# One RWKV block on one core: new landing estimates in a hand-built plan, and a new order of all pieces

## The chip, the cores and the metric

One NeuronCore of one Trainium2 chip. The time is that of one execution of the whole program on the device, in microseconds; lower is better. The core's engines are TensorE (PE, its weight loads are listed as PEld), VectorE (DVE), ScalarE (ACT), GpSimd (POOL) and SyncE (SP), which here only issues transfers.

## The reference, cut to what matters

Eight sequences (`b`) of 256 tokens with 512 channels (32 heads of 16) go through one RWKV block, in float32:

```python
xn = _ln(x, ln1_w, ln1_b);  sx = _token_shift(xn, state[:, i1])
xxx = jnp.tanh((xn + sx * maa_x) @ maa_w1).reshape(b, l, 5, 1, EXTRA_MAA)
xxx = jnp.matmul(xxx, maa_w2).reshape(b, l, 5, E)
x5 = xn[:, :, None] + sx[:, :, None] * (maa_stack + xxx)
w = jnp.exp(-jnp.exp(time_decay + jnp.tanh(x5[:, :, 1] @ decay_w1) @ decay_w2))
r, k, v = x5[:, :, 3] @ Wr.T, x5[:, :, 0] @ Wk.T, x5[:, :, 2] @ Wv.T
g = jax.nn.silu(x5[:, :, 4] @ Wg.T)
def step(s, rkvw):                       # over the 256 tokens
    a = k_t[:, :, :, None] * v_t[:, :, None, :]
    out = jnp.einsum('bhk,bhkd->bhd', r_t, u * a + s)
    return (a + w_t[:, :, :, None] * s, out)
att = group_norm(outs) * gn_w + gn_b
x = x + att * g @ Wo.T
xn2 = _ln(x, ln2_w, ln2_b);  sx2 = _token_shift(xn2, state[:, i0])
rr = jax.nn.sigmoid((xn2 + sx2 * ffn_maa_r) @ ffn_Wr.T)
kk = jnp.square(jax.nn.relu((xn2 + sx2 * ffn_maa_k) @ ffn_Wk.T))
return x + rr * (kk @ ffn_Wv.T)
```

## The kernel before, in words

The program is a list of 2,633 **pieces** of work, each of a few instructions on one engine: 397 for PE, 1,132 for ACT, 479 for DVE, 374 for POOL and 251 transfers. For every sequence the pieces come in three stages. `inputs_of_scan` normalizes the input, transposes it (L614), mixes it with the shifted one (`psx`, the small `tanh` part and the mixing matmuls `psm`, whose results DVE and POOL turn into five mixed inputs at L716, L720 and L726) and makes the projections k, v, r and g (`psk`, `psv`, `psr`, `psg`, by `project`, all matmuls through `mul` at L430) and the decay (`psd` at L766, `psw`). `scan` runs the recurrence in four blocks of heads with four quarters each. For a quarter the values come back broadcast from DRAM (`vs<-vo`; `vo` is written by two small transfers on ACT's queue at L816 for sequence 0 and by one at L866 for the others), DVE multiplies them with k (L889; POOL at L886 for a few), DVE scans (L891), POOL multiplies with r (L894), and PE sums the four quarters of a block into one tile, `pat`, which is called the gather below (L902; 32 matmuls that begin with one of each quarter). `rest` makes the group norm (squares at L920, means `pv` at L928, logarithm and exponential on ACT at L933 and L935, for the last sequence a spread by matmuls at L943), the gate (L959, L968), the output projection `pso` with the residual on DVE (L974), the second layer norm (L556, L595, L598) with its transposes `psT2` (L614), and the two feed-forward projections `psfk`, `psfr` and `psfv` (ACT at L983, L984, L992; DVE at L1015; POOL's last sum at L1020).

The order is not written out in the functions. Each piece is added with a cost and, for a transfer, with a time on the wire and a lag until it has landed (`EARLY` for named first transfers, `LANDS` by kind, else a default). `sequence` gives each piece its rank from the table `TURNS`, one number for each piece, stage by stage. `order` then takes the pieces by rank as soon as what they need is placed, gives each the latest-freed fitting buffer out of its pool, and works out starts from the costs; the pieces are emitted sorted by these starts, and each engine executes its own in that order. So a landing figure moves no transfer by itself: it changes the starts that `order` works out, and by them the sorting and the buffers. All transfers go through `dma` (L419) on SP's queue, except the writes of `vo`. Six tiles of PSUM (`ps`) serve all projections, gathers and transposes. ACT has two sets of function tables, one with the exponential and one with tanh and silu; where a piece needs the other set, L1048 puts a table load ahead of it.

The lines that speak of landings are these:

```python
op.wire, op.lag = self.EARLY.get(name) or self.LANDS.get("".join(c for c in name if not c.isdigit()), (kb / 370, 1.5))
...
landed = wire = max(wire, op.start + 1.0) + op.wire
...
o.ready = max(o.ready, op.end + op.gap if same else landed + op.lag + self.AHEAD.get(o.engine, 0.0))
```

Of the kernel before, what the change touches and what calls it, by code (L numbers as in the profile page):

```python
# [70 lines left out]
class Plan:  # L71
# [7 lines left out]
    EARLY = {"xt0_0": (0.76, 0.8), "xt0_1": (0.76, 0.8), "cen": (0.35, 1.5), "vec": (0.2, 1.5), "xt1": (1.4, 1.5), "xt2": (1.4, 1.5), "Wfr0_1": (1.4, 1.5),  # L79
             "Wraw0": (1.65, 1.5), "Wraw1": (1.65, 1.5)}  # L80
# [23 lines left out]
    def add(self, engine, us, outs, ins, emit, mode=None, into=(), lag=0.0, kb=0, part=False):  # L104
# [7 lines left out]
        if kb:  # L112
            name = op.bufs[0].name
            op.wire, op.lag = self.EARLY.get(name) or self.LANDS.get("".join(c for c in name if not c.isdigit()), (kb / 370, 1.5))

# [17 lines left out]
    def stage(self):  # L133
# [990 lines left out]
```

## Time and profile before

| | before |
|---|---|
| median of three runs | 608.50 us (608.11, 608.50, 608.68) |
| the profiled execution, its own time | 608.87 us |
| its span from the first to the last instruction | 607.1 us |
| busy: PE, DVE, ACT, POOL | 597.6, 531.2, 513.3, 505.4 us |
| bytes moved, mean rate | 124.85 MB, 206 GB/s |
| granted clock of TensorE | 1.00 throughout |

The profile's page gives busy time and shares of the span for each engine, then the chain of work that ended last, then the costliest groups of instructions. The timeline lists instructions in order of time; in brackets stands how long the engine sat idle before one, and what released it. "SPq" and "ACTq" are transfers issued by these engines.

### The profile page before, as it was taken

The numbers are of one execution on the slowest core, as the hardware profiler recorded it, in microseconds if no ns is written. First come the engines' busy times: TensorE is split into PE (matmuls) and PEld (weight loads), VectorE is DVE, ScalarE is ACT, GpSimd is POOL, SyncE is SP. The second block draws the span as 40 slices with busy tenths as digits, with TensorE's granted clock in tenths as the row PEclk, the third lists the DMA queues.
The fourth block names the chain that finished last, engine by engine and source line by source line (L and its number), as shares of the span: only waits on it lengthen the run. The fifth ranks groups of instructions, "written<-read, shape, count | busy, mean of one in ns | idle before, by whom it ended". The sixth has DMA issues, their size and how long they took to land.

```text
span 607.1 us, 18838 instructions
## 1 busy us (share of the span) xinstructions
PE 597.6 (98%) x7892; PEld 344.4 (57%) x7892; DVE 531.2 (87%) x481; ACT 513.3 (85%) x1199; POOL 505.4 (83%) x385
## 2 busy tenths in 40 slices
PE   8999999999999999999999999999999999999997
PEld 7575655467444574377544774465644454745464
DVE  6699999899999989799798999999999999994332
ACT  4898879999999999999999999999998688963431
POOL 1699999999989897899979898989989989887030
PEclk9999999999999999999999999999999999999999
DMA  9796688898778868486589597795876798961551
GB/s 292 251 246 163 143 205 207 223 263 219 205 210 252 231 189 231 138 233 174 164 256 238 143 270 219 225 228 148 271 212 174 204 252 220 265 194 43 177 185 65
DMA packets 52500, 124.85 MB, mean 206 GB/s; under 512 B 5824, under 2 KB 11200, under 8 KB 52416
## 3 DMA queue, kind: packets, MB, share of 16 engines
q1 hardware_dynamic: 48048, 119.46, 71.8%
q10 hardware_dynamic: 4368, 4.20, 2.2%
q8 instruction: 62, 1.02, 0.7%
q14 instruction: 22, 0.18, 0.1%
HBM read 115.25 MB, written 8.39 MB: 204 GB/s over the span
## 4 chain that ended last, share of the span: by engine, by line
PE 88%; ACT 6%; DMA 4%; DVE 2%; issue 1%; SPq 0%; DVEq 0%; ACTq 0%
PE ps L430 73%; PE ps L902 9%; PE ps L614 2%; PE ps L766 2%; DMA Wk<-in_wk 2%; ACT ps L714 1%; DMA mw2a<-in_maa_w 1%; ACT sq L957 1%; DMA x<-in_x 1%; PE ps L928 1%; ACT L1048 1%; PE ps L844 1%; ACT rk L957 1%; ACT mix L984 0%; DVE x L974 0%
## 5 line engine op out<-in xcount | busy, mean ns | idle before, releaser
L891 DVE TENSOR_TENSOR_SCAN st<-wrep,vs 128x1024 f32<-128x1024 f32 x128 | 288.9, 2279 | 4.3 <-ACT wrep L872 2.2
L894 POOL TENSOR_TENSOR st<-st,r 128x1024 f32<-128x1024 f32 x128 | 254.2, 2002 | 11.3 <-DVE st L891 10.4
L889 DVE TENSOR_TENSOR vs<-vs,ps 128x1024 f32<-128x1024 f32 x122 | 144.6, 1208 | 9.3 <-ACT vs L882 6.5
L430 PE MATMUL ps<-Ws,mix 128*32 128x512 f32 (+2 forms) x804 | 114.7, 589 | 0.5 <-DVE x L974 0.2
L430 PEld LDWEIGHTS ps<-Ws,mix 128*32 128x32 f32 (+1 forms) x804 | 38.8, 118 | 62.7 <-issue 55.6
L726 POOL TENSOR_TENSOR mix<-mix,xn 128x512 f32<-128x512 f32 x62 | 67.0, 1096 | 7.7 <-DVE mix L720 6.8
L902 PE MATMUL ps<-st,con 128*32 128x256 f32 x1024 | 62.6, 380 | 0.3 <-DVE x L974 0.2
L430 PE MATMUL ps<-mix,Wg 128*32 128x256 f32 (+1 forms) x784 | 60.2, 379 | 0.3 <-ACT mix L983 0.2
L430 PE MATMUL ps<-mix,Wv 128*32 128x256 f32 (+1 forms) x832 | 59.9, 380 | 0.2 <-DVE mix L723 0.2
L430 PE MATMUL ps<-mix,Wr 128*32 128x256 f32 (+1 forms) x688 | 59.9, 380 | 0.0
L430 PE MATMUL ps<-mix,Wk 128*32 128x256 f32 (+1 forms) x880 | 59.4, 380 | 0.2 <-DMA Wk<-in_wk 0.2
L430 PE MATMUL ps<-mix,Ws 128*32 128x256 f32 (+1 forms) x784 | 58.2, 379 | 0.0
L430 PE MATMUL ps<-Ws,g 128*32 128x512 f32 (+1 forms) x416 | 57.1, 593 | 0.0
L1048 ACT ACT_TABLE_LOAD x39 | 50.0, 1283 | 1.1 <-ACT v L797 0.4
L647 POOL TENSOR_TENSOR mix<-mix,xn 128x512 f32<-128x512 f32 x44 | 47.2, 1093 | 3.1 <-ACT mix L645 2.9
L430 PEld LDWEIGHTS ps<-mix,Wr 128*32 128x32 f32 (+1 forms) x688 | 39.3, 123 | 17.9 <-issue 1.4
L714 ACT ACTIVATE ps<-ps,vec 128x256 f32<-128x256 f32 x112 | 45.7, 445 | 4.2 <-PE ps L430 2.7
L430 PEld LDWEIGHTS ps<-mix,Wv 128*32 128x32 f32 (+1 forms) x832 | 37.9, 116 | 19.5 <-issue 1.1
L902 PEld LDWEIGHTS ps<-st,con 128*32 128x32 f32 x1024 | 34.1, 110 | 26.3 <-issue 5.1
L430 PEld LDWEIGHTS ps<-mix,Ws 128*32 128x32 f32 (+1 forms) x784 | 39.6, 118 | 16.4 <-DVE mix L640 0.6
L430 PEld LDWEIGHTS ps<-mix,Wg 128*32 128x32 f32 (+1 forms) x784 | 38.4, 118 | 18.2 <-issue 1.0
L430 PEld LDWEIGHTS ps<-mix,Wk 128*32 128x32 f32 (+1 forms) x880 | 36.8, 114 | 20.6 <-issue 2.4
(116 smaller groups left out, 935.3 us busy)
## 6 DMA issues: line engine op xcount, KB each, us to landing
vs<-vo SPq DMA_DIRECT2D x128, 512.0 KB, 5.6
Ws<-in_wo SPq DMA_DIRECT2D x16, 512.0 KB, 6.6
Ws<-in_fr SPq DMA_DIRECT2D x16, 512.0 KB, 6.0
Ws<-in_fk SPq DMA_DIRECT2D x16, 512.0 KB, 5.6
Ws<-in_fv SPq DMA_DIRECT2D x16, 512.0 KB, 4.7
x<-in_x SPq DMA_DIRECT2D x9, 512.0 KB, 6.4
vo<-v ACTq DMA_DIRECT2D x15, 256.0 KB, 4.9
out<-o SPq DMA_DIRECT2D x15, 256.0 KB, 4.6
```

Source lines behind the costliest of these rows:

```text
L430: nc.tensor.matmul(out[i : i + n], lhsT=w[:, i : i + n], rhs=x, start=first, stop=final)
L614: nc.tensor.transpose(ps()[:, m, n * P : (n + 1) * P], xh[n]()[:, k * P : (k + 1) * P], idt())
L647: gp(512, t, [t, xn[q]], lambda q=q, t=t: nc.gpsimd.tensor_tensor(t(), t(), xn[q]()[:, :, 1 : T + 1], ALU.add))
L714: act(256, p_, [p_, vec], lambda g=g, q=q, m=m, p_=p_: nc.scalar.activation(p_()[:, m, :], p_()[:, m, :], AF.Identity, bias=col(f"maa_{g}" ...
L726: gp(512, t, [t, xn[q]], lambda q=q, t=t: nc.gpsimd.tensor_tensor(t(), t(), xn[q]()[:, :, 1 : T + 1], ALU.add))
L766: nc.tensor.matmul(pd()[i : i + 32, 0, :], lhsT=w, rhs=src[k // 2]()[:, k % 2, :], start=(k == begin), stop=(k == end))
L889: dve(4 * T, [vs], [vs, kp], lambda m=m, vs=vs, kp=kp: nc.vector.tensor_tensor(vs(), vs(), kp()[:, m : m + 1, :].to_broadcast([P, 4, T]), ...
L891: dve(4 * T, [st], [w, vs], lambda w=w, vs=vs, st=st: nc.vector.tensor_tensor_scan(st().rearrange("p n t -> p (n t)"), w().rearrange("p n ...
L894: gp(4 * T, st, [st, r], lambda m=m, st=st, r=r: nc.gpsimd.tensor_tensor(st(), st(), r()[:, m : m + 1, :].to_broadcast([P, 4, T]), ALU.mul ...
L902: nc.tensor.matmul(pat()[32 * i : 32 * i + 32, 0, :], lhsT=con()[:, s : s + 32], rhs=done[i]()[:, j, :], start=(j == 0), stop=(j == 3),)
L957: act(256, rsb, [rs], lambda blk=2 * q + n, n=n, rows=rows, rsb=rsb: nc.scalar.copy(by_block(rsb)[rows, n, :], rs()[32 * blk : 32 * blk + ...
L1048: nc.scalar.preload_act_table_set(TABLES[table])
```

## The change

Landing figures of the first transfers are set anew, and the whole table of ranks is replaced. Pieces, costs, pools and buffers stay as they were.

```diff
-    EARLY = {"xt0_0": (0.76, 0.8), "xt0_1": (0.76, 0.8), "cen": (0.35, 1.5), "vec": (0.2, 1.5), "xt1": (1.4, 1.5), "xt2": (1.4, 1.5), "Wfr0_1": (1.4, 1.5),
-             "Wraw0": (1.65, 1.5), "Wraw1": (1.65, 1.5)}
+    EARLY = {"xt0_0": (0.76, 1.28), "xt0_1": (0.76, 1.2), "cen": (0.35, 2.1), "vec": (0.2, 2.3), "xt1": (1.4, 2.3), "xt2": (1.4, 2.0), "idt": (0.17, 2.4), "Wfr0_1": (1.4, 1.5),
+             "Wraw0": (1.65, 2.1), "Wraw1": (1.65, 2.0)}
...
-            op.wire, op.lag = self.EARLY.get(name) or self.LANDS.get("".join(c for c in name if not c.isdigit()), (kb / 370, 1.5))
+            op.wire, op.lag = self.EARLY.get(name) or self.LANDS.get("".join(c for c in name if not c.isdigit()), (kb / 370, 2.0))
...
     TURNS = """
-        11 45 15 38 49 98 95 96 109 46 94 72 220 97 55 62 64 140 16 14 26 20 27 43 18 54 58 17 40 48 19 60 61,
+        3 66 13 39 57 92 67 93 99 69 58 68 70 198 107 108 120 121 9 18 24 21 32 44 19 60 61 20 30 43 33 51 55,
...
```

Three places show what the new ranks do. First SP's queue at the head of the program; names are the destinations (`Wk_74` and `Wk_73` are the two halves of the k weights, `xt_85` the input of sequence 1, `vs` the first broadcast values). Before, from the twelfth transfer on:

```order
L419 DMA mw2a<-in_maa_w 128x512
L419 DMA s_81<-in_state 128x64
L419 DMA s_82<-in_state 128x64
L419 DMA xt_85<-in_x 128x2x512
L419 DMA Wr_78<-in_wr 128x2x512
L419 DMA Wr_77<-in_wr 128x2x512
L419 DMA dw_69<-in_decay_w 128x4x64
L419 DMA dw_70<-in_decay_w 128x512
L419 DMA Wg_80<-in_wg 128x2x512
L419 DMA mw2b<-in_maa_w 128x512
L419 DMA Wk_73<-in_wk 128x2x512
L419 DMA vs_144<-vo_141 128x1x1024
```

Now, from the same place:

```order
L419 DMA mw2a<-in_maa_w 128x512
L419 DMA Wr_77<-in_wr 128x2x512
L419 DMA xt_85<-in_x 128x2x512
L419 DMA con<-in_consts 128x448
L419 DMA dw_69<-in_decay_w 128x4x64
L419 DMA Wr_78<-in_wr 128x2x512
L419 DMA Wk_74<-in_wk 128x2x512
L419 DMA Wg_79<-in_wg 128x2x512
L419 DMA mw2b<-in_maa_w 128x512
L419 DMA dw_70<-in_decay_w 128x512
L419 DMA Wk_73<-in_wk 128x2x512
L419 DMA vs_144<-vo_141 128x1x1024
```

The twenty-two transfers ahead of the first `vs` are the same kinds and sizes in both orders; the first half of Wk goes from eleventh to eighteenth, and the second half stays last.

Second, PE ahead of the gather of sequence 1's second block, after which the transposes of sequence 0's second layer norm stand (the sixteen rows L902 are the 32 matmuls of the gather, then eight rows L614 follow). Before:

```order
L430 MATMUL ps_174<-w_133,dw_70 32x256 x4
L430 MATMUL ps_169<-w_133,dw_70 32x256 x4
L430 MATMUL ps_174<-w_133,dw_70 32x256 x4
L430 MATMUL ps_169<-w_133,dw_70 32x256 x4
L430 MATMUL ps_170<-mix_119,Wk_73 32x256 x8
L430 MATMUL ps_170<-mix_112,Wk_74 32x256 x8
L902 MATMUL ps_172<-st_152,con 32x256
L902 MATMUL ps_172<-st_154,con 32x256
L902 MATMUL ps_172<-st_155,con 32x256
```

Now:

```order
L430 MATMUL ps_173<-w_133,dw_70 32x256 x4
L430 MATMUL ps_170<-w_133,dw_70 32x256 x4
L430 MATMUL ps_173<-w_133,dw_70 32x256 x4
L430 MATMUL ps_170<-w_133,dw_70 32x256 x4
L430 MATMUL ps_169<-mix_119,Wk_73 32x256 x8
L430 MATMUL ps_169<-mix_117,Wk_74 32x256 x8
L430 MATMUL ps_171<-mix_108,Wv_75 32x256 x8
L430 MATMUL ps_171<-mix_107,Wv_76 32x256 x8
L902 MATMUL ps_169<-st_152,con 32x256
L902 MATMUL ps_169<-st_154,con 32x256
L902 MATMUL ps_169<-st_155,con 32x256
```

One half of a v projection (`mix` by `Wv`), which stood behind the transposes, now stands ahead of the gather; gather and transposes follow each other as before.

Third, POOL ahead of the gather of sequence 4's second block, which needs the four products L894 of that block (the last of the four is the last row of each piece). Before:

```order
L858 TENSOR_TENSOR att_140<-v_128,att_140 128x2x256
L726 TENSOR_TENSOR mix_107<-mix_107,xn_98 128x512
L959 TENSOR_TENSOR att_138<-att_138,rk_150 128x2x256
L968 TENSOR_TENSOR g_136<-att_139,g_136 128x512
L968 TENSOR_TENSOR g_137<-att_138,g_137 128x512
L726 TENSOR_TENSOR mix_110<-mix_110,xn_98 128x512
L894 TENSOR_TENSOR st_152<-st_152,r_125 128x1024
L726 TENSOR_TENSOR mix_108<-mix_108,xn_98 128x512
L726 TENSOR_TENSOR mix_106<-mix_106,xn_99 128x512
L726 TENSOR_TENSOR mix_112<-mix_112,xn_99 128x512
L858 TENSOR_TENSOR att_138<-v_129,att_138 128x2x256
L894 TENSOR_TENSOR st_153<-st_153,r_125 128x1024
```

Now:

```order
L726 TENSOR_TENSOR mix_108<-mix_108,xn_99 128x512
L968 TENSOR_TENSOR g_137<-att_138,g_137 128x512
L959 TENSOR_TENSOR att_139<-att_139,rk_150 128x2x256
L726 TENSOR_TENSOR mix_106<-mix_106,xn_99 128x512
L968 TENSOR_TENSOR g_136<-att_139,g_136 128x512
L726 TENSOR_TENSOR mix_107<-mix_107,xn_98 128x512
L894 TENSOR_TENSOR st_153<-st_153,r_127 128x1024
L726 TENSOR_TENSOR mix_110<-mix_110,xn_99 128x512
L1020 TENSOR_TENSOR o_163<-o_163,x_160 128x512
L1020 TENSOR_TENSOR o_162<-o_162,x_160 128x512
L726 TENSOR_TENSOR mix_117<-mix_117,xn_98 128x512
L894 TENSOR_TENSOR st_152<-st_152,r_127 128x1024
```

Two of the last sums of an earlier sequence (L1020) and one mixing sum more (L726) now stand ahead of the block's last product, and of the two multiplications by v (L858) one has gone ahead of this stretch and one behind it. On PE one half of a projection that stood ahead of this gather stands behind it now.

## Rows read from the trace of the kernel before

**Rows 1.** The page: busy time by engine, and the chain's shares by engine.
```profile
PE 597.6 (98%) x7892; PEld 344.4 (57%) x7892; DVE 531.2 (87%) x481; ACT 513.3 (85%) x1199; POOL 505.4 (83%) x385
...
PE 88%; ACT 6%; DMA 4%; DVE 2%; issue 1%; SPq 0%; DVEq 0%; ACTq 0%
```
**Rows 2.** Stretches: from:to, length, busy (count) PE PEld DVE ACT POOL, clock, DMA, GB/s.
```profile
0.00:25.00 25.00, 21.63 (x196) 17.29 (x200) 17.28 (x41) 15.25 (x39) 8.44 (x19) 1.00 0.88 293
...
60.00:90.00 30.00, 30.00 (x592) 18.15 (x588) 30.00 (x25) 23.03 (x51) 29.91 (x19) 1.00 0.71 173
...
540.00:607.00 67.00, 62.88 (x479) 34.64 (x478) 28.34 (x38) 24.43 (x49) 23.28 (x19) 1.00 0.36 126
```
**Rows 3.** Stretches of the head, same columns.
```profile
12.00:15.00 3.00, 2.89 (x22) 2.27 (x29) 2.00 (x8) 2.87 (x5) 0.00 (x0) 1.00 1.07 369
```
**Rows 4.** The chain that ended last, by time: start, us, what.
```profile
15.39 9.36 DMA Wk<-in_wk
...
210.72 3.45 PE ps L430 x64
...
318.19 1.93 PE ps L902 x32
```
**Rows 5.** Timeline of the head, PE and ACT's queue: start, us, engine line.
```profile
7.52 1.06 PE L614 MATMUL ps<-idt,xh 128*128 128x128 f32 x8 [0.97 <-DMA idt<-in_consts]
...
24.86 0.40 PEld L430 LDWEIGHTS ps<-mix,Wk 128*32 128x32 f32 x12 [0.68 <-POOL mix L726]
24.89 0.64 PE L430 MATMUL ps<-mix,Wk 128*32 128x256 f32 x8 [0.22 <-DMA Wk<-in_wk]
...
22.38 0.35 ACTq L816 DMA_DIRECT2D vo<-v  x1
```
**Rows 6.** Timeline at sequence 0's second layer norm.
```profile
128.51 2.52 PE L902 MATMUL ps<-st,con 128*32 128x256 f32 x32
129.11 1.43 PEld L902 LDWEIGHTS ps<-st,con 128*32 128x32 f32 x26 [0.48 <-POOL st L894]
129.24 1.52 ACT L598 ACTIVATE xh<-x,nm,rs 128x512 f32<-128x512 f32 x2
...
130.96 1.09 PE L614 MATMUL ps<-idt,xh 128*128 128x128 f32 x8
```
**Rows 7.** Timeline ahead of the gather of sequence 4's second block, POOL, DVE and PE.
```profile
313.34 1.09 POOL L959 TENSOR_TENSOR att<-att,sq 128x512 f32<-128x512 f32 x1 [2.07 <-ACT sq L957]
...
318.62 1.09 POOL L858 TENSOR_TENSOR att<-v,att 128x512 f32<-128x512 f32 x1 [0.27 <-ACT att L852]
...
323.55 1.09 POOL L968 TENSOR_TENSOR g<-att,g 128x512 f32<-128x512 f32 x1 [0.57 <-ACT att L963]
...
331.81 2.01 POOL L894 TENSOR_TENSOR st<-st,r 128x1024 f32<-128x1024 f32 x1
...
328.13 0.68 DVE L1015 SCALAR_TENSOR_TENSOR o<-o,ps 128x512 f32<-128x512 f32 x1
...
336.61 1.72 PE L902 MATMUL ps<-st,con 128*32 128x256 f32 x28
```
**Rows 8.** Table loads on ACT: the page's group, then the timeline of the last sequence's norm.
```profile
L1048 ACT ACT_TABLE_LOAD x39 | 50.0, 1283 | 1.1 <-ACT v L797 0.4
...
559.18 0.47 ACT L933 ACTIVATE sq<-ps,eh 128x256 f32<-128x256 f32 x1 [1.00 <-PE ps L928]
...
559.69 0.42 ACT L935 ACTIVATE sq<-sq 128x256 f32<-128x256 f32 x1
...
560.76 0.73 PEld L943 LDWEIGHTS ps<-sq,con 64*128 64x128 f32 x8 [0.84 <-ACT sq L935]
```
**Rows 9.** Who waited for whom on PE: total us, times, longest.
```profile
PE ps L614 <- DVE xh L588: 0.5, 1, 0.5
PE ps L430 <- DVE mix L716: 0.4, 1, 0.4
PE ps L430 <- ACT k L797: 0.3, 1, 0.3
```

236 rows, old and new, of the table TURNS are left out of this document.

## The prediction, made before the changed kernel was run

> **What bounds the kernel now.** I read the page first, then stretches of the span, then the chain, then the timeline where the order changes.
>
> The page says that PE is busy for 597.6 of 607.1 us, and that the chain of work that ended last runs through PE for 88% [rows 1]. The other engines are at 83 to 87%. So PE's stream of matmuls is the bound, and an order can only win or lose what PE waits. The 9.5 us in which PE is idle lie mostly at the two ends: 3.4 us in the first 25 us and 4.1 us in the last 67 us [rows 2]; the 515 us between hold 2.0 us. That is not all PE loses, because a wait for operands inside a group is partly booked as busy. The pace without waits is seen in 64 matmuls that take 3.45 us, and in a gather of 32 after which the next group starts 1.93 us later [rows 4]. A place where it takes longer is a stall.
>
> In the first 90 us there is a second bound. DVE is busy for 30.00 of the 30 us from 60 to 90 [rows 2], with the scans of sequence 0. What PE gained ahead of them it would wait for again at the gathers.
>
> The head is bound by transfers. From 12 to 15 us the queues move 369 GB/s at a DMA share of 1.07 [rows 3]; the second half of Wk, issued at 15.39, is in flight for 9.36 us [rows 4], and at 24.89 PE starts the k projection, for which it last waited on that landing, while its weight load waited 0.68 us for a mixing sum of POOL [rows 5].
>
> The sum is made against the profiled execution: 608.87 us, of which 607.1 are span and 1.77 lie around it. It stands 0.37 us above the median of 608.50; the change that I work out is applied to the median.
>
> **The change, part by part.**
>
> *The landing figures themselves: nothing.* They are arithmetic in the planner. No transfer is issued, sized or queued differently because of them; only the order that comes out counts.
>
> *PE's amount of work: nothing.* Both orders have 1,375 rows on PE, with the same pieces, and both change tile shape 82 times.
>
> *The head: nothing, bounds -0.3 and +0.7 us.* The same twenty-two transfers stand ahead of the broadcasts, and the second half of Wk stays last, so behind a saturated queue it lands when all these bytes have. Moved ahead are idt, the centering constant and vec, smaller and earlier. The first transposes waited 0.97 us for idt [rows 5] and may come some tenths sooner, but PE's pieces up to the k projection are the same set, and that projection still waits for the last transfer. What is won before it is waited for there. The gain ends where the mixing sum of POOL ends, 0.3 us earlier at most: the weight load at 24.86 was free to go only then. The loss side is another queue. Two writes of `vo` of 128 KB go out on ACT's queue, the first at 22.38 [rows 5]. In the new order the two halves of the v projection that feed them stand next to each other, so both can be issued about a microsecond earlier, into the last bytes of Wk: 2 x 128 KB at 369 GB/s is 0.7 us if they go wholly first, nothing if they go behind. I take nothing, the nearer end by the row: the first write was issued 2.4 us ahead of that landing before as well. "DMA: Bandwidth & Descriptors", section "Queues, rings and completion order", of the Trainium skill says that each DMA engine takes turns between its queues packet by packet, so the writes would not stand behind Wk; by it an estimated half of the 0.7 us would be lost, and no row of the trace before shows the two side by side.
>
> *The scans of sequence 0: nothing.* DVE is the bound there [rows 2], and it has the same work ahead of the last of these scans in both orders.
>
> *Sequence 0's second layer norm: -0.4 us, bounds -0.5 and +0.3.* The gather starts at 128.51; its next weight loads wait 0.48 us for POOL's last product, and the transposes behind it start at 130.96 [rows 6]. That is 2.45 us where 1.93 are needed [rows 4], so 0.52 us are lost. Now half a v projection, 32 of the matmuls that take 3.45 us for 64, so 1.73 us, stands ahead of the gather. POOL has one multiplication by v more ahead of its last product, 1.09 us by the same line in [rows 7], so product and gather still come within tenths of each other; and the normalized rows that the transposes need, ready at 129.24 + 1.52 = 130.76 [rows 6], are pushed by about 1 us by POOL's small sum and by an eviction on ACT, to about 131.9, against the 132.2 at which PE now gets there. Most of the 0.52 comes back; if POOL is late by another half microsecond, nothing does and 0.3 is lost.
>
> *Sequence 4's second gather: +0.5 us, bounds 0 and +0.9.* POOL's last product ended at 331.81 + 2.01 = 333.82 and the gather started at 336.61, 2.79 us later [rows 7]. In the new order PE arrives 1.73 us earlier, at 334.88, since half a projection has moved behind. POOL has two L1020 and one L726 more, one L858 less between its start at 313.34 and that product: 2 x 1.09, less overlap of neighbours, is 2.1 us. It sat idle for 0.27 and 0.57 us on the way [rows 7]. If both idles are filled, the product ends at 333.82 + 2.1 - 0.84 = 335.08 and PE loses 0.2 us, or nothing if it is itself late by then; if neither, it ends at 335.9 and PE loses about 1. The 0.57 stands behind a scaling on ACT that the change moves little, so I take the middle, 0.5.
>
> *Other gathers: +0.1 us, bounds 0 and +0.5.* Where DVE or POOL has more work ahead of a gather than before, it is by less than the product's lead there, except near sequence 6's last gather, where lead and extra work about match.
>
> *Two more table loads on ACT: nothing, bounds 0 and +0.4 us.* Before there are 39 behind the first, 1.283 us each, with only 1.1 us of idle in front of all of them [rows 8]. The two that come to them lie in the last 55 us, where ACT is busy for 24.4 of 67 us [rows 2]. One stands on a short chain: between the last squares and L933. The exponential L935 ends at 560.11 and PE's matmuls of L943 start at 560.76, after the projection that runs until then [rows 8]. ACT was idle for 1.00 us ahead of L933 [rows 8], which takes up all but 0.3 of the load's 1.28; L935 then ends 0.3 us later, and the 0.65 us cover it.
>
> *Waits that stay.* The layer norm of sequence 7 on DVE (0.5 us), the mixing result of sequence 1 (0.4) and an eviction of k (0.3) [rows 9] have the same neighbours on PE in both orders. The tail has the same pieces in the same order.
>
> Sum: 0 - 0.4 + 0.5 + 0.1 + 0 = +0.2 us. **Forecast: 608.5 + 0.2 = 608.7 us**, no difference that can be measured: a measurement of this kernel tells about 0.2%, 1.2 us, from no change. Its own range, by the bounds that can come together, is 607.6 to 609.8.
>
> **The rivals.**
>
> *Faster: the new order takes the short waits out, chance 0.25.* The order is spread over 164 of PE's 397 positions, and I priced only where cover shrinks or a known wait moves. If the 0.5 at the layer norm and the three waits of rows 9, 0.5 + 0.4 + 0.3, all go and the two gathers cost nothing, that is -1.7 us, 606.8. For it: POOL and DVE queues elsewhere have been reshuffled more than I can follow row by row. Against it: the three waits keep their neighbours.
>
> *Slower: POOL is late for sequence 4's gather, chance 0.13.* The two L1020 now stand in front of the block's last product, and they add what DVE's L1015 writes. DVE did the second of these at 328.13 to 328.81 [rows 7], and POOL would reach it at 313.34 plus ten small operations and three products, about 330.5. From the point at which DVE is 1.7 us later with L1015 than before, each further microsecond goes straight through POOL's queue into PE. At 3 us later that is 1.3 us on top of the 0.9 of the upper bound: 608.5 - 0.4 + 0.9 + 1.3 = 610.3 us. For it: POOL's lead was the only reserve, and PE now comes earlier. Against it: DVE has spare time in this part of the span, and L1015 has not moved far.
>
> *The vo writes cut into the last weight, chance 0.05.* The k projection starts at 25.2 to 25.6 instead of 24.89: +0.5 us on the sum, 609.2, still within what counts as no difference. Part of it is given back, since DVE's scans wait on other chains.
>
> *A table load holds ACT for longer than its own row, chance 0.05.* The load ahead of L933 takes 1.28 us, of which the idle leaves 0.3 open, and PE's projection then covers 0.65. If ACT stood for twice the time, L933 would start 1.28 us later again, and PE would miss 0.3 + 1.28 - 0.65 = 0.9 us at L943: 608.7 + 0.9 = 609.6; with the bound of +0.9 at the gather it is 610.0, slower. Against it: ACT idled for 1.1 us in all in front of 39 loads [rows 8]. "ScalarE: Activation LUTs", section "What ACT_TABLE_LOAD costs", of the Trainium skill gives ~1283 ns for the load, as the row has it, and ~1380 ns more for a drain; by it this case would be the rule, with the sum at 609.7.
>
> **How the numbers follow.** The forecast has 0.52 and the vo writes 0.05: together 0.57 for within 0.2%. Faster by more than 0.2% has 0.25. Slower by more has 0.13 + 0.05 = 0.18. The range reaches to 606.6, just under the faster rival, and to 610.2, into the two slower ones; what lies outside is about a tenth on each side.
>
> **What would show it.** Right: k starts at 24.7 to 25.2; the 32-matmul gather ahead of sequence 0's transposes is followed after 1.9 to 2.1 us; PE waits 0.2 to 0.9 us for POOL at sequence 4's second gather; PE busy stays at 597 to 598 us. Wrong: a gather of sequence 4 or 6 that waits over 1 us for L894, with an idle of POOL in front of L1020; L943 released by L935 with PE idle; or PE idle between 25 and 540 us of well under 2.0 us together with shorter gathers, which would be the faster rival.

## The result, and the profile after

| | before | changed |
|---|---|---|
| median, the executions beside each other | 608.73 us (607.95 to 610.42, 16) | 610.44 us (608.94 to 611.63, 16) |
| ratio, with its 95% interval | | 1.0024 (1.0015 to 1.0033) |
| span of the profiled execution | 607.1 us | 607.6 us |
| its own time | 608.87 us | 609.49 us |

The changed kernel is slower by 0.24%, just over the 0.2% that the prediction set as the bound. From the predicted base of 608.5 the ratio gives 610.0 us, inside the range of 606.6 to 610.2, 1.3 us above the forecast of 608.7, and on the side that had a chance of 0.18. It is outside the narrower range of 607.6 to 609.8 that the terms gave by their own bounds.

One thing must be known to read these times. Executions of this program, of either kernel, come at two levels, by the mean clock that TensorE was granted over the span: 0.999 to 1.000 (full clock below), or 0.993 to 0.997 (the lower clock). Of the changed kernel's sixteen, eight lie at either level, with medians of 609.50 and 611.48 us. In three later sets of executions of the kernel before, 51 of 104 were at full clock, median 608.69, and 53 below it, 610.00. Set beside these, the changed kernel is 0.8 us slower at full clock and 1.5 us slower at the lower one. (The sixteen executions of the kernel before that ran beside it have no clock on record; the full-clock medians of the three later sets differ by 0.3 us among themselves, and differences between sets are uncertain by about that much.) Medians over a whole set move with the share of the two levels; the levels are compared apart below.

The page of the changed kernel, busy time and the chain's shares, answers to [rows 1]:

```profile
PE 597.4 (98%) x7928; PEld 338.3 (56%) x7928; DVE 531.4 (87%) x481; ACT 516.1 (85%) x1201; POOL 506.7 (83%) x385
...
PE 81%; ACT 11%; DVE 3%; issue 1%; DMA 1%; POOL 1%; SPq 0%; ACTq 0%; DVEq 0%
```

PE's busy time is what it was; the chain now runs through ACT, DVE and POOL more often. Who waited for whom on PE in the changed kernel (total us, times, longest):

```profile
PE ps L430 <- DMA Ws<-in_wv: 1.5, 1, 1.5
...
PE ps L430 <- DVE mix L723: 1.0, 1, 1.0
PE ps L430 <- issue: 0.8, 2, 0.4
```

The first two waits are in the head, and the third is in the tail. Of [rows 9] only the wait for L588 is left, 0.46 us at 577.63; the other two, 0.4 and 0.3 us, are gone. The timeline of the head on PE. First one line of the kernel before that [rows 5] leaves out, then the changed kernel:

```profile
20.81 1.99 PE L430 MATMUL ps<-mix,Wv 128*128 128x256 f32 x8 [0.18 <-DVE mix L723]
```

```profile
6.74 1.14 PE L614 MATMUL ps<-idt,xh 128*128 128x128 f32 x8 [0.20 <-DVE xh L588]
9.38 3.19 PE L430 MATMUL ps<-Ws,Ws 128*128 128x128 f32 x24 [1.50 <-DMA Ws<-in_wv]
...
20.84 2.86 PE L430 MATMUL ps<-mix,Wv 128*128 128x256 f32 x12 [1.03 <-DVE mix L723]
...
25.38 1.91 PE L430 MATMUL ps<-mix,Wk 128*32 128x256 f32 x32
```

idt lands earlier and the transposes start 0.8 us earlier. But the first half of the v weights is issued at 3.57 us instead of 2.62, PE waits for it, and starts on it at 9.38. Before, it waited at this place for the centering constant until 9.31, so the 0.8 us are lost again. At 20.84 PE has waited 1.03 us for a mixing sum, with four v matmuls done and twelve still to do; before, eight were done, and the wait was 0.18. The k projection starts at 25.38 instead of 24.89, and it no longer waits for the last weight: PE itself is late.

The two gathers of the prediction, from the timeline of the changed kernel (PE and ACT at sequence 0's layer norm, then POOL and PE at sequence 4's second gather), answer to [rows 6, 7]:

```profile
130.78 1.52 ACT L598 ACTIVATE xh<-x,nm,rs 128x512 f32<-128x512 f32 x2
130.80 1.91 PE L902 MATMUL ps<-st,con 128*32 128x256 f32 x32
132.64 1.09 PE L614 MATMUL ps<-idt,xh 128*128 128x128 f32 x8
...
312.24 1.10 POOL L959 TENSOR_TENSOR att<-att,sq 128x512 f32<-128x512 f32 x1 [4.23 <-ACT sq L957]
...
329.11 2.14 POOL L1020 TENSOR_TENSOR o<-o,x 128x512 f32<-128x512 f32 x2
...
332.26 2.00 POOL L894 TENSOR_TENSOR st<-st,r 128x1024 f32<-128x1024 f32 x1
...
335.03 1.91 PE L902 MATMUL ps<-st,con 128*32 128x256 f32 x32
```

Gather to transposes is now 1.84 us, so the stall is gone. At the other gather POOL ended at 334.26, 0.77 us ahead of PE: no wait.

The tail is where the profiled execution lost most. First the kernel before, POOL, DVE and PE at sequence 7's second layer norm, then the same lines of the changed kernel:

```profile
578.62 1.09 POOL L1020 TENSOR_TENSOR o<-o,x 128x512 f32<-128x512 f32 x1 [20.64 <-DVE o L1015]
581.52 1.66 DVE L640 SCALAR_TENSOR_TENSOR mix<-sx,vec,xn 128x256 f32<-128x256 f32 x4
582.37 1.82 PE L430 MATMUL ps<-mix,Ws 128*128 128x256 f32 x7
```

```profile
580.64 1.54 POOL L1020 TENSOR_TENSOR o<-o,x 128x512 f32<-128x512 f32 x1
581.15 2.50 DVE L640 SCALAR_TENSOR_TENSOR mix<-sx,vec,xn 128x256 f32<-128x256 f32 x4
582.56 1.66 PE L430 MATMUL ps<-mix,Ws 128*128 128x256 f32 x5 [0.40 <-issue]
```

In the new order POOL makes the shift of sequence 7 (L628) ahead of sequence 6's sum (L1020). The sum then runs from 580.64 to 582.18, beside DVE's mixing. The four L640 take 2.50 us together instead of 1.66, and PE, which came to the transposes ahead of them 0.38 us earlier than before (577.63 against 578.01), starts the feed-forward matmuls 0.19 us later. The same line by single instructions (minimum, median and maximum, ns), of the kernel before and of the changed kernel:

```profile
L640 DVE SCALAR_TENSOR_TENSOR mix<-sx,vec,xn x4: 472/472/473, 581.5 to 582.7; 128x256 f32<-128x256 f32 x4
```

```profile
L640 DVE SCALAR_TENSOR_TENSOR mix<-sx,vec,xn x4: 473/474/1309, 581.1 to 583.2; 128x256 f32<-128x256 f32 x4
```

One of the four takes 1309 ns. It is the first, which runs from 581.15 to 582.46, so it ends 0.28 us after POOL's sum; the other three take about 474. "Advanced Engine Details and Errata", section "GPSIMD Details", of the Trainium skill says that POOL shares a read and a write interface with DVE and conflicts with DVE instructions of two SBUF inputs, which L640 is (`sx` and `xn`); the 1309 ns agree.

### The profile page after: what moved, and what is told of

Its sections match the earlier page's. It is cut to its first block, busy times and chain, and to the rows that moved or that the text cites. A ratio compares the mean times of both kernels' runs of the same rounds, so it can differ in the third digit from the quotient of the medians.

```text
span 607.6 us, 18920 instructions
## 1 busy us (share of the span) xinstructions
PE 597.4 (98%) x7928; PEld 338.3 (56%) x7928; DVE 531.4 (87%) x481; ACT 516.1 (85%) x1201; POOL 506.7 (83%) x385
## 4 chain that ended last, share of the span: by engine, by line
PE 81%; ACT 11%; DVE 3%; issue 1%; DMA 1%; POOL 1%; SPq 0%; ACTq 0%; DVEq 0%
PE ps L430 68%; PE ps L902 8%; PE ps L614 2%; PE ps L766 2%; ACT ps L714 1%; ACT L1048 1%; DVE st L891 1%; ACT att L852 1%; DMA Ws<-in_wv 1%; ACT mix L645 1%; ACT wrep L872 1%; ACT vs L882 1%; ACT xh L598 1%; POOL st L894 1%; PE ps L928 1%
## 5 line engine op out<-in xcount | busy, mean ns | idle before, releaser
L894 POOL TENSOR_TENSOR st<-st,r 128x1024 f32<-128x1024 f32 x128 | 254.3, 2003 | 9.8 <-DVE st L891 8.3
L726 POOL TENSOR_TENSOR mix<-mix,xn 128x512 f32<-128x512 f32 x62 | 67.5, 1104 | 13.6 <-DVE mix L720 8.1
L902 PE MATMUL ps<-st,con 128*32 128x256 f32 x1024 | 61.7, 381 | 0.0
L628 POOL TENSOR_TENSOR sx<-xn 128x512 f32<-128x512 f32 x30 | 31.4, 1056 | 34.3 <-ACT xn L624 34.2
L852 ACT COPY att<-ps 32x256 f32<-32x256 f32 x128 | 46.6, 364 | 3.0 <-PE ps L844 0.9
L430 PEld LDWEIGHTS ps<-mix,Ws 128*32 128x32 f32 (+1 forms) x832 | 36.9, 116 | 19.7 <-issue 1.2
```

The costliest lines, as they stand in the source:

```text
L430: nc.tensor.matmul(out[i : i + n], lhsT=w[:, i : i + n], rhs=x, start=first, stop=final)
L628: take(512, [sx], [xn], lambda xn=xn, sx=sx, e=nc.vector if alone and q else nc.gpsimd: e.tensor_tensor(sx(), xn()[:, :, 0:T], xn()[:, :, ...
L726: gp(512, t, [t, xn[q]], lambda q=q, t=t: nc.gpsimd.tensor_tensor(t(), t(), xn[q]()[:, :, 1 : T + 1], ALU.add))
L852: act(350, atts[q], [pc], lambda i=32 * (2 * q + m), m=m, q=q, h=32 * h: nc.scalar.copy(atts[q]()[h : h + 32, m, :], pc()[i : i + 32, 0, :]))
L894: gp(4 * T, st, [st, r], lambda m=m, st=st, r=r: nc.gpsimd.tensor_tensor(st(), st(), r()[:, m : m + 1, :].to_broadcast([P, 4, T]), ALU.mul ...
L902: nc.tensor.matmul(pat()[32 * i : 32 * i + 32, 0, :], lhsT=con()[:, s : s + 32], rhs=done[i]()[:, j, :], start=(j == 0), stop=(j == 3),)
```

## The experiments

All of them are the changed kernel or the kernel before with pieces moved in the table of ranks, or with matmuls added. A moved piece is shown by the rows of its engine. Times at full clock are medians of the executions whose mean granted clock is 0.999 or 1.000. Each set of four ran beside 34 or 35 executions of the kernel before; their medians at full clock were 608.74, 608.55 and 608.82 us.

### One half of a v projection moved back, in the head

```diff
 L430 MATMUL mix,Wv  x2   (first group, first half)
+L430 MATMUL mix,Wv  x2   (second group, first half)
 L430 MATMUL mix,Wv  x2   (first group, second half: waits for L723)
-L430 MATMUL mix,Wv  x2   (second group, first half)
```

With this piece two of the six tiles `ps` exchange their roles from there to the end; the order of no other piece changes.

> The changed kernel with one PE piece moved: the first half of the second v matmul group of sequence 0 stands ahead of the second half of the first again, as in the kernel before. Theory (the halves cost the head): PE has 8 matmuls by Wv ahead of its wait for the mixing sum L723 at about 20.8 us instead of 4, so the k projection starts at 24.8 to 25.0 instead of 25.38 and the first scan on DVE at about 32.6 instead of 33.11; if DVE's scans hand this on, the span is 0.3 to 0.6 us shorter than the changed kernel's 607.6. Rival (the head is given back later anyway): k starts earlier, the span stays within 0.2 us. Rival (con, which lands at 16.5 instead of 12.3 and pushes L552 in between DVE's mixing): the first scan stays at 33.0 or later.

Measured: 609.43 us at full clock (8 of 12), against 609.50 of the changed kernel; over all 1.0012 (0.9998 to 1.0026) against the kernel before. The profiled execution was one at the lower clock, so its k projection, at 26.44, can't be set beside 25.38. Its wait for L723 is 0.16 us instead of 1.03, as the theory says. That the head is given back later, the first rival, is what the time says; the start at full clock was seen in later runs with the same order, below.

### POOL's sum moved back, in the tail

```diff
+L1020 TENSOR_TENSOR o_162<-o_162,x_160 128x512
 L628 TENSOR_TENSOR sx_104<-xn_99 128x512
-L1020 TENSOR_TENSOR o_162<-o_162,x_160 128x512
```

> The changed kernel with one POOL piece moved in the tail: the sum L1020 of sequence 6 stands ahead of the shift L628 of sequence 7 again, as before. Theory (POOL's sum beside DVE's mixing L640 slows both): the four L640 take 1.66 us together instead of 2.50, the feed-forward matmuls of sequence 7 run without their two waits (0.55 and 0.42 us), and the span is 0.8 us shorter than the changed kernel's: 606.8. Rival (the table load that now stands ahead of L992 and L645 on ACT is what PE waits for): no change of the span, within 0.2 us.

Measured: span 606.6, and 608.75 us at full clock (7 of 12), 0.75 below the changed kernel. DVE's line by single instructions in its profile:

```profile
L640 DVE SCALAR_TENSOR_TENSOR mix<-sx,vec,xn x4: 471/472/472, 581.1 to 582.3; 128x256 f32<-128x256 f32 x4
```

And POOL, DVE and PE in its timeline:

```profile
578.16 1.09 POOL L1020 TENSOR_TENSOR o<-o,x 128x512 f32<-128x512 f32 x1 [20.72 <-DVE o L1015]
...
581.06 1.66 DVE L640 SCALAR_TENSOR_TENSOR mix<-sx,vec,xn 128x256 f32<-128x256 f32 x4
581.91 2.47 PE L430 MATMUL ps<-mix,Ws 128*128 128x256 f32 x10
```

The theory holds: no other engine's program differs from the changed kernel's, the table load is still in its place on ACT (579.43), and the loss is gone. Over all the median is 610.19, because five of twelve fell to the lower clock.

### Both moves

> The two moves of the other two kernels together. If both theories hold and add: span 606.2 to 606.5, and a time 1.1 to 1.4 us below the changed kernel's 610.4, that is about the time of the kernel before. If the head is given back later: 0.8 us below. If neither matters: no change against the changed kernel.

Measured: 608.54 us at full clock (5 of 12), 0.96 below the changed kernel and 0.2 below the kernel before beside it; seven of twelve at the lower clock (610.44). The two moves undo the change's loss at full clock, by a little less than the 1.1 to 1.4 expected. The profiled execution fell on the lower clock, and its span of 608.2 doesn't test the span that was expected.

### The table load moved away

```diff
 L992 ACTIVATE o_162 (sequence 6, first tile)
+L992 ACTIVATE o_163 (sequence 6, second tile)
 L556, L558, L617, L624 ... (sequence 7's layer norm)
-L1048 ACT_TABLE_LOAD
-L992 ACTIVATE o_163 (sequence 6, second tile)
 L645 ... L984 (sequence 7's feed-forward)
+L1048 ACT_TABLE_LOAD
```

> The changed kernel with one ACT piece moved in the tail: the tanh L992 of sequence 6's second tile stands directly behind that of the first tile, ahead of sequence 7's layer norm, which saves two table loads. Theory (POOL's sum is the cause, not the table load): the four L640 still take 2.5 us, and the span stays within 0.2 us of 607.6. Rival (the table load at 579.5 is on the path): the span is 0.5 to 0.9 us shorter.

Measured: 609.48 us at full clock (7 of 12), as the changed kernel. No load is saved: the program has 41 behind the first, as the changed kernel, and the one that stood at 579.51 now stands at 592.48. It is gone from the place in question all the same, and there the four L640 take 2.50 us as in the changed kernel. (A few pieces of the tail also get other tiles `ps`.) The span is 608.2, outside the 0.2 us that were expected, but PE was already 0.6 us late when it came to the transposes of this layer norm (578.23 instead of 577.63). The table load is not the cause. The other load, ahead of L933, did what the prediction said: in the changed kernel L935 ended at 559.98 and PE's L943 started at 560.39, after its projection.

### The clock in the head

The profiles of two of these runs, of the v halves and of both moves, fell on the lower clock. Stretches of 1 us of the first, columns as in [rows 2] (the clock stands third from the end):

```profile
8.00:9.00 1.00, 0.00 (x0) 0.00 (x0) 1.00 (x3) 0.83 (x2) 0.09 (x1) 1.00 1.01 309
9.00:10.00 1.00, 0.28 (x1) 0.32 (x2) 0.98 (x3) 0.00 (x0) 0.95 (x1) 0.71 1.03 386
10.00:11.00 1.00, 1.00 (x6) 1.00 (x6) 1.00 (x4) 0.38 (x2) 0.00 (x0) 0.50 1.13 368
11.00:12.00 1.00, 1.00 (x7) 1.00 (x7) 1.00 (x4) 0.21 (x2) 0.20 (x1) 0.50 1.11 350
...
13.00:14.00 1.00, 1.00 (x11) 1.00 (x11) 0.00 (x0) 0.74 (x2) 0.00 (x0) 1.00 1.05 387
```

PE's wait for the v weights in the same run, and in the run with both moves:

```profile
9.71 4.40 PE L430 MATMUL ps<-Ws,Ws 128*128 128x128 f32 x24 [1.95 <-DMA Ws<-in_wv]
...
9.58 4.54 PE L430 MATMUL ps<-Ws,Ws 128*128 128x128 f32 x24 [1.79 <-DMA Ws<-in_wv]
```

In the first run PE stands still until 9.71. The granted clock falls at about 9.4, while PE still waits, to 0.50, the lower level of 1.2 GHz, and stays there until about 12.8 us. In the second it falls at about 9.7, 0.1 us after PE has gone on, and stays there until about 13.1. Six or seven matmul instructions fit a microsecond instead of nine to eleven. Four kernels fill this wait with matmuls on a zero operand that nobody reads, so they compute more than the reference asks for:

```diff
+                if u == "1_0" and q == 0:
+                    for _ in range(6):
+                        nc.tensor.matmul(plan.pools["ps"][-1][1][:, 0, 0:P], lhsT=hm().rearrange("p k j -> p (k j)"),
+                                         rhs=hm().rearrange("p k j -> p (k j)"), start=True, stop=True)
```

> The changed kernel with 6 matmuls more on PE, by the same zero operand as the first twelve, behind the first transposes of sequence 0: work whose result nobody reads, put where PE now waits 1.5 us for the v weights. In the profiles of two other runs PE's granted clock stood at 0.50 from about 9.7 to 13 us, right behind that wait, and half of the changed kernel's executions had a mean clock of 0.996 to 0.998. Theory (the idle time lets the clock fall): with PE busy there, at most 2 of 12 executions have a mean clock under 0.9985, and the median is that of the executions at full clock, 609.5. Rival (the clock falls whatever PE does there): 4 or more of 12 at the lower clock, median 610 or more. Rival (the six run at half speed and are late): k projection 0.3 to 1 us later, 610.

Measured, the changed kernel with the six: none of 11 executions below 0.999, median 609.84. The clock stays up, as the theory says; the median is 0.3 above the changed kernel's at full clock and above the 609.5 expected. In the profile the v weights are taken up at 9.97 instead of 9.38 and k starts at 25.70 instead of 25.38. It isn't separated whether this is the price of the six or a later landing: in the profiles of the new order PE takes up these weights anywhere between 9.26 and 10.14. The same stretches of its profile:

```profile
8.00:9.00 1.00, 1.00 (x11) 1.00 (x10) 1.00 (x3) 1.00 (x2) 0.00 (x0) 1.00 0.93 340
...
10.00:11.00 1.00, 1.00 (x9) 1.00 (x10) 1.00 (x3) 0.20 (x2) 0.13 (x1) 1.00 1.11 349
```

The six in PE's timeline, two instructions each, where it waited before:

```profile
7.79 1.50 PE L617 MATMUL ps<-hm 128*128 128x128 f32 x12
```

> The kernel with both moves (v halves in the head, POOL's sum in the tail) and the same 6 matmuls. If the clock stays up and the moves hold: median 608.4 to 608.6, under the kernel before's 609.1 on this chip. If the clock falls as often as without: median 609.9 as without the six.

Measured, both moves and the six: none of 11 at the lower clock, median 608.37, ratio 0.9991 (0.9981 to 1.0001) against the kernel before. In its profile the k projection starts at 24.57, 0.8 us earlier than in the changed kernel. The order of the v halves does what the first experiment expected of it, with luck on top, since PE could take up the v weights at 9.26 here.

> The changed kernel with POOL's sum moved in the tail and the 6 matmuls in the head, the v halves left as changed. Against the variant that has both moves and the six (608.37), this tells what the order of the v halves is worth at full clock. Theory (the head's delay is taken up by sequence 0's scans, on which PE waits anyway): 608.4 to 608.8, within 0.4 us of it. Rival (the head counts in full): 608.9 to 609.2.

Measured, POOL's sum moved and the six, the v halves left as changed: 608.70 us, all 12 at full clock. Its k projection starts at 25.36, 15.74 us after PE took up the v weights; in the run above it was 15.31, so the v halves move k by about 0.4 us, and the rest of the 0.8 between the two profiles is when the weights came. By the two medians the halves are worth 0.3 us. By the ratios to the kernel before beside each run, 0.9989 (0.9980 to 0.9998) here and 0.9991 above, they are worth nothing that can be told. Set beside the run with the six alone (609.84), POOL's sum is worth 1.1.

> The new order with both moves, the 6 matmuls behind the first transposes and 2 more at the start. Expected as without the two: no execution at the lower clock, median 608.2 to 608.5, under the kernel before's median of 609.1 to 609.3 on this chip. If the two at the start make the first transposes late: 0.1 to 0.4 us more.

Measured: none of 12 at the lower clock, but a median of 609.02, above what was expected; the ratio, 0.9990 (0.9981 to 0.9999), is about that of the run without the two. They gained nothing. In this profile PE took up the v weights 0.9 us later than in the other (at 10.14), the latest of all the profiles. I did not find out why.

### The kernel before, filled in the same way

> The kernel before with 3 such matmuls behind its first transposes, where PE waits 0.7 us. Theory (idle time there lets the clock fall): at most 2 of 12 executions under 0.9985, median 608.7. Rival (the clock falls for another reason): 4 or more of 12, median 609.0 to 609.3 as without.

Measured: 4 of 12 at the lower clock, against 16 of 34 of the kernel before beside it, median 609.05. This is what the rival gave: filling this wait alone did not keep the clock up. Whether idle time elsewhere lets it fall was open still, because PE's longer wait, ahead of the first transposes, was left, 1.75 us in its profile.

> The kernel before with 4 matmuls more at the very start (16 instead of 12) and 2 behind the first transposes, so that PE's idle time ahead of the transposes (1.0 to 1.75 us in the profiles) is filled too. Theory (a PE that idles for well over a microsecond in the head, and then starts, may find its clock at half): at most 2 of 12 executions under 0.9985, where the kernel before has 31 of 69 on this chip and the one before it and the variant with 3 matmuls behind the transposes alone had 4 of 12; median 608.6. Rival (the kernel before loses its clock somewhere else): 4 or more of 12, median 609.0 or more.

Measured: none of 12 at the lower clock, against 22 of 35 beside it; median 608.59 (608.02 to 609.23), ratio 0.9983 (0.9973 to 0.9994). PE in the head of its profile:

```profile
1.05 6.69 PE L488 MATMUL ps<-hm 128*128 128x128 f32 x32 [1.05 <-DVE hm L486]
7.95 1.06 PE L614 MATMUL ps<-idt,xh 128*128 128x128 f32 x8 [0.21 <-DMA idt<-in_consts]
8.85 0.61 PE L617 MATMUL ps<-hm 128*128 128x128 f32 x4
9.71 1.47 PE L430 MATMUL ps<-Ws,Ws 128*128 128x128 f32 x11 [0.26 <-DMA Ws<-in_consts]
```

With six matmuls that cost PE 0.4 us of the head, the old order is faster than both kernels of this study, and by its ratio about as fast as the new order with both moves and six such matmuls (0.9991).

### The old head with the new middle

> The first 260 pieces of the new order, sorted as in the kernel before (transfers, DVE's L552 and all), then the rest of the new order with POOL's sum moved as in the second experiment. What the new middle is worth without the new head and tail. Theory (the middle gains, as the trace shows PE's lag falling from 0.9 behind to 0.4 ahead between 70 and 510 us): executions at full clock at 607.9 to 608.4, against 608.74 of the kernel before. Rival (the fall is only the head's delay being absorbed): 608.7, as before. The clock is low as often as in the kernel before, in 4 to 6 of 12.

Measured: 608.61 us at full clock (9 of 12), against 608.55 beside it; three at the lower clock, one fewer than expected. The rival holds: the middle is worth nothing by this measure. The lag of one profile behind another, worked out from PE's starts at the same amount of matmul work, shows why the trace had looked otherwise. At the middle of sequence 0's scans the changed kernel is 0.8 us behind the kernel before, at their end 0.2, and this run, 0.5 us ahead before these scans, is 0.1 behind after them. PE waits there for DVE, whatever it had won or lost. How early PE comes to the tail also differs without any change of the order ahead of it: sequence 7's transposes start at 578.01 in the kernel before and at 577.62 in the next run, which has its order up to there, so the 577.63 of the changed kernel shows no gain.

### POOL's sum moved late in the kernel before

```diff
+L628 TENSOR_TENSOR sx_103<-xn_101 128x512
 L1020 TENSOR_TENSOR o_163<-o_163,x_160 128x512
-L628 TENSOR_TENSOR sx_103<-xn_101 128x512
```

> The kernel before with one POOL piece moved, the reverse of the second experiment: the shift L628 of sequence 7 ahead of the sum L1020 of sequence 6. Theory (POOL's sum then runs beside DVE's first L640 and holds it): the first L640 takes about 1.3 us instead of 0.47, and the time at full clock is 0.7 to 0.85 us above the kernel before's. Rival: POOL's sum ends before DVE gets to L640 and nothing changes, within 0.2 us.

Measured: 609.08 us at full clock (6 of 12) against 608.82 beside it, and 610.84 against 610.17 at the lower clock. DVE's line by single instructions:

```profile
L640 DVE SCALAR_TENSOR_TENSOR mix<-sx,vec,xn x4: 469/470/1309, 581.1 to 583.2; 128x256 f32<-128x256 f32 x4
```

POOL and PE in the timeline of the same run:

```profile
580.62 1.54 POOL L1020 TENSOR_TENSOR o<-o,x 128x512 f32<-128x512 f32 x1
...
582.50 3.86 PE L430 MATMUL ps<-mix,Ws 128*128 128x256 f32 x15 [0.36 <-DVE mix L640]
```

The mechanism is the same: only POOL's program differs, and the slowest L640 takes 1309 ns, as in the changed kernel, instead of 473. The time rose by 0.3 and 0.7 us, less than the 0.7 to 0.85 expected at full clock; with six executions at each level that differ by a microsecond among themselves, the times leave the size open. The traces don't. PE's transposes of sequence 7's second layer norm, just ahead of the place, first in the kernel before, then in this run:

```profile
578.01 1.09 PE L614 MATMUL ps<-idt,xh 128*128 128x128 f32 x8 [0.46 <-DVE xh L588]
```

```profile
577.62 1.09 PE L614 MATMUL ps<-idt,xh 128*128 128x128 f32 x8 [0.46 <-DVE xh L588]
```

From there to the end of the span it is 29.1 us before (of 607.1) and 29.9 here (of 607.5). All the profiles agree: 29.0 to 29.1 us in the nine where POOL's sum stands ahead of the shift, and 29.9 to 30.0 in the five where it stands behind, the changed kernel among them. So the sum's place is worth 0.8 us in the tail.

## Why the prediction was right or wrong

- **The bound.** Right: PE's busy time is the same within 0.2 us, the landing figures alone issue nothing (with the old ranks and the new figures the program has the same rows on every engine), and at full clock the whole effect is in what PE waits.
- **The head, priced at nothing with -0.3 and +0.7.** The size was inside the bounds, the reason was wrong. "PE's pieces up to the k projection are the same set, and that projection still waits for the last transfer" took PE's order within the set as free. It was not: with the v halves adjacent, PE reached its wait for L723 with half the work in front, and k came 0.49 us later without waiting for Wk. I saw that the halves had become adjacent and used it only for the `vo` writes; the second of those went out later (24.41 instead of 23.58), not earlier. That k's start fell into the 25.2 to 25.6 of the rival on the `vo` writes is chance, since k did not wait for Wk. The time of this loss is small, 0.3 us at most in the runs here, because sequence 0's scans take most of it up, as the prediction's second bound says.
- **Sequence 0's layer norm, -0.4.** Right in place, and in the trace 2.45 us became 1.84, a little more than the bound of 0.5. That the time took it is not shown: the run with the old head and the new middle gained nothing.
- **Sequence 4's gather, +0.5.** Wrong, within its bounds: nothing. The step that failed is POOL's start. It began at 312.24 instead of 313.34, since the work ahead of it came earlier, and that 1.1 us paid for half of the longer queue; of the two idles of 0.27 and 0.57 on the way, one of 0.27 was left. With it the slower rival falls: L1015 was done by 326.98, and POOL reached the sums without a wait.
- **The table loads, nothing.** Right. The estimate of 1 us late at L943 by a drain on top of the load did not show, neither there, where L933 starts 0.01 us after its load's 1.28 us have passed (557.76 to 559.05), nor in the tail when a load was moved away.
- **"Waits that stay."** One of three did. The wait for L588 (0.46 us) is in both profiles; the mixing result (0.4) and the eviction of k (0.3) no longer hold PE in the changed kernel. So part of the faster rival came in the trace, and none of it in the time, as far as the run with the new middle tells.
- **The tail, "the same pieces in the same order".** This is the step that cost the forecast. It holds for PE and not for POOL, whose sum had moved by one place behind the shift, next to DVE's mixing. It was in the order of the changed kernel for anyone who read POOL's queue at that place. Moving it back gave 0.75 us at full clock, nearly all of the 0.8 by which the changed kernel is slower there, and the traces give 0.8 for it.
- **The range.** It held 610.0 by luck. Its upper end, 610.2, came from two slower rivals, POOL late at sequence 4's gather and ACT held by a table load, and neither happened; what made the kernel slower had no term and no rival.
- **The clock.** Not in the prediction at all: the profile before showed 1.00 throughout, and one profile at full clock says nothing of how many executions are. In the changed kernel a fall costs 2.0 us (609.50 to 611.48), in the kernel before 1.3 (608.69 to 610.00). So the forecast left out two things, the 0.8 us of the tail and what the falls add to a median over all executions. Falls are about as frequent in both orders, 29 of 64 and 53 of 104 executions where nothing is filled. Why the cost differs was not settled, since no profile of the kernel before fell on the lower clock.

## What to carry to other kernels

When a table reorders a whole program, read every engine's queue at the places where the bound has no slack, above all the tail: a sum moved by one place on POOL held a DVE instruction that PE was waiting for. Price a reordering within a set of pieces by what stands in front of each wait, not by the set. And look at the spread of the executions with their granted clocks before reading differences of a microsecond: here six matmuls that nobody needs, in the waits of the head, were worth more than the new order of 2,633 pieces.

## What the runs showed of the hardware

A granted clock of 1.00 in one profile hid that about half of the executions have a lower mean clock. The two profiles that caught one show 3.4 us of the head at 0.50; no profile of the kernel before did. In the one PE had stood still for 1.95 us for a transfer, and the clock fell 0.3 us before it went on; in the other it had stood for 1.79 us, and the clock fell 0.1 us after. But waits of 1.4 to 1.75 us in the head of profiles at full clock did not lead to it, so what decides is open. With matmuls in these waits, none of 58 executions fell (46 of the new order, 12 of the old); with only the shorter wait of the old order filled, 4 of 12 did. A POOL sum beside DVE instructions with two inputs took 1.54 us instead of 1.09, and the one that started while it ran took 1.31 us instead of 0.47.
